# Cross-attention in 160 slots: the path of the probabilities from block transposes to key rows, and the buffers of z and x

## The chip, the cores and the metric

The kernel runs on one core of a Trainium2 chip. The metric is device microseconds (us) of one execution. A profile of one execution stands beside it; its span runs from the core's first to its last instruction.

## The reference

`x` holds 32 batches of 512 rows (queries) by 640 channels, `ctx` holds 32 batches of 77 rows (keys) by 1024. There are 20 heads of 32 channels. The other three key groups of the reference (object, others, ip) begin behind row 77, so they are empty here and add nothing. What is left:

```
q = heads(x @ to_q_w); k = heads(ctx @ to_k_w); v = heads(ctx @ to_v_w)
p = softmax(q @ k.T / sqrt(32)); a = merge(p @ v)
out = a @ to_out_w + to_out_b + x
```

All inputs and outputs are float32.

## The kernel before, in words

**Precision.** The large products (queries, keys, values, output) run in the faster fp32r form. Each operand is split into a high part (cast, ScalarE) and a low part (difference, VectorE or GpSimd), and three products (high-high, high-low, low-high; `PAIRS`) are summed. Scores and probabilities times values run in plain fp32.

**Stages.** First come 12 products of zeros (`warm`, line 253) while the first weights arrive. Then keys and values of all batches are computed in five groups of context rows and stored to DRAM (`k_dram`, `v_dram`). Then the main part runs as 160 slots: slot n is batch b = n // 5 and channel chunk j = n % 5, that is four heads of one batch. `end()` closes the last batches.

**One slot** (`slot`, line 573). The order on each engine is the order in which the program writes the instructions (a manual schedule), so each engine and the DMA-issuing queue of SyncE (SP) go through their own list in order, and an instruction that waits holds up all behind it on that engine.

- TensorE: `scores(n)` (line 410, `sc`), `values(n-3)` (line 478, `pa` from `raw` and `vb`), a piece of the output projection (line 515, `po`), `queries(n+1)` (line 393, `pq`), a second piece of the projection. Batch 0 and slots 5 and 6 have no projection pieces (`has_out` is false); slots 0 to 6 are called the filling here.
- VectorE: `maxima` (line 422), `transpose_p(n-1)` (line 454), additions of the residual (line 544), block transposes of x (line 235), the reciprocal of the sums (line 442), the low part of `pa` (line 497).
- ScalarE: 16 exponentials with sums (line 432, `pn`), the high part of `pa`, the copy of `pq` (line 402), the high parts of x (line 242).
- GpSimd: bias (line 508), normalization of `pn` (line 447), the low parts of x (line 243).

**The way of the probabilities.** `pn` holds queries in the partitions. The values product needs keys in the partitions. `transpose_p(n-1)` turns 32x32 blocks with VectorE into the one buffer `z`: partition 32a+i of `z` holds row i of every block, for the queries of block a. A row of 80 columns per head does not begin at a multiple of 32, so blocks straddle heads. Four transfers on SP (line 461, 160 KB each) write `z` to a DRAM buffer `pd` (`pd<-z`). One slot later `load_p` (line 470) reads it back with one 640 KB transfer (`raw<-pd`), whose 80 partitions are the keys. `raw` has two buffers and is read by `values` a slot after that.

**The way of x.** `load_x` (line 231) loads a batch in four transfers of 320 KB into `xs`, of which there is one buffer. Slots j = 0 and 1 of a batch turn the next batch's `xs` in place (line 235), slots j = 2 and 3 split it into `xt` (lines 242 and 243; seven buffers of one chunk each). In the steady part the load of batch b+2 stands at the end of that, in slot j = 4, since it has to wait until the splits have read `xs`. On SP it stands ahead of that slot's stores of `z`.

Of the kernel before, what the change touches and what calls it, by code (L numbers as in the profile page):

```python
# [8 lines left out]
F32 = mybir.dt.float32  # L9
# [14 lines left out]
P = 128  # L24
Q = 32
# [1 line left out]
HD = 32  # L27
NKEY = 77
HPC = 4
KPAD = 80  # L30
NBLK = HPC * KPAD // Q

# [3 lines left out]
def kernel(  # L38
# [43 lines left out]

    k_dram = dram.tile([P, NC_, NT], F32, name="k_dram")

    v_dram = dram.tile([NT + KPAD - NKEY, NC_, HPC, HD], F32, name="v_dram")
    wo_dram = dram.tile([P, NC_, 2, C], FPR, name="wo_dram")

    def split(hi, lo, src):
# [135 lines left out]
    def load_x(b, quarters=range(4)):  # L224

        if b not in xss:
            xss[b] = xpool[0].tile([P, S // Q, C // 4], F32, tag="xs", name="xs")
        xs = xss[b]
        src = x[b].rearrange("(a j) (q u) -> q j a u", j=Q, q=4)
        for q in quarters:  # L230
            nc.sync.dma_start(xs[q * Q : (q + 1) * Q, :, :], src[q])  # L231

    def transpose_x(b, i):
        part = xss[b][:, 4 * i : 4 * i + 4, :].rearrange("p a u -> p (a u)")
        nc.vector.transpose(part, part)  # L235

    def split_x(b, c, high=nc.scalar.copy, low=nc.gpsimd):

        xt = xpool[0].tile([P, 2, S], FPR, tag="xt", name="xt", bufs=7)
        src = xss[b].rearrange("p (a t) u -> p t a u", t=NQ)[:, :, :, c * Q : (c + 1) * Q]  # L240
        parts = [xt[:, i, :].rearrange("p (t a j) -> p t a j", t=NQ, j=Q) for i in range(2)]
        high(parts[0], src)  # L242
        low.tensor_tensor(parts[1], src, parts[0].bitcast(F32), ALU.subtract)  # L243
        xts[b, c] = xt
# [4 lines left out]
    zero = kvt.tile([P, G], FPR, name="zero")  # L249
    nc.vector.memset(zero.bitcast(F32), 0.0)  # L250
    warm = psk.tile([P, G], F32, tag="ps", name="warm")
    for _ in range(12):
        nc.tensor.matmul(warm, zero[:, :P], zero, start=True, stop=True)

    def first(*ks):
# [38 lines left out]
    def split_wo():  # L294
# [6 lines left out]
    load_context(1, NK)  # L301
    nc.sync.dma_start(
        v_dram[NT:].rearrange("n j i d -> (n j i d)").rearrange("(p u) -> p u", p=P),
        zero[:, : (KPAD - NKEY) * HEADS * HD // P].bitcast(F32),
    )
    for g in range(LAST):
        for j in range(NC_):
# [54 lines left out]


    main = ctx.enter_context(tc.tile_pool(name="main", bufs=1, reuse_waits="tile"))
    ps = ctx.enter_context(tc.tile_pool(name="ps", bufs=1, space=PSUM, reuse_waits="tile"))
    psv = tc.alloc_tile_pool(name="psv", bufs=3, space=PSUM, side="right", reuse_waits="tile")
    late = []

    raws, ats, pds, sms, pqs, pas, xrs, pos, scs, nms, rss = ({} for _ in range(11))

    bias = main.tile([P, C], F32, name="bias")
    nc.sync.dma_start(bias, bo.unsqueeze(0).to_broadcast([P, C]))
    kbs = [main.tile([P, NC_, NKEY], F32, name=f"kb{n}") for n in range(2)]
    vbs = [main.tile([KPAD, NC_, HPC, HD], F32, name=f"vb{n}") for n in range(2)]
    pnb = []
    for n in range(2):
        pn = main.tile([P, NQ * HPC, KPAD], F32, name=f"pn{n}")
        nc.gpsimd.memset(pn, 0.0)
        pnb.append(pn)
    qts = [main.tile([P, S], F32, name=f"qt{n}") for n in range(2)]  # L380
    z = main.tile([P, NBLK, NQ, Q], F32, name="z")
    def load_keys(b):
        nc.sync.dma_start(kbs[b % 2], k_dram[:, :, b * NKEY : (b + 1) * NKEY])

    def load_values(b):
        nc.sync.dma_start(vbs[b % 2], v_dram[b * NKEY : b * NKEY + KPAD])

    def queries(n):
        b, j = divmod(n, NC_)
        pqs[n] = ps.tile([P, S], F32, tag="pq", name="pq", bufs=1)  # L390
        for k in range(NC_):
            for m, (a, c) in enumerate(PAIRS):
                nc.tensor.matmul(  # L393
                    pqs[n],
                    wq_s[:, k, a, j * P : (j + 1) * P],
                    xts[b, k][:, c, :],
                    start=(k == 0 and m == 0),
                    stop=(k == NC_ - 1 and m == 2),
                )
# [37 lines left out]
                accum_out=sms[n][:, at : at + 1],  # L437
            )

    def sums(n):  # L440
        rss[n] = main.tile([P, NQ * HPC], F32, tag="rs", name="rs", bufs=2)
        nc.vector.reciprocal(rss[n], sms.pop(n))  # L442

    def normalize(n):
        rs = rss.pop(n)
        pf = pnb[n % 2][:, :, :NKEY]
        nc.gpsimd.tensor_tensor(  # L447
            pf, pf, rs.unsqueeze(2).to_broadcast([P, NQ * HPC, NKEY]), ALU.mult
        )

    def transpose_p(n):

        pn = pnb[n % 2]
        nc.vector.transpose(  # L454
            z.rearrange("p b t j -> p t b j"),
            pn.rearrange("p (t h) k -> p t (h k)", t=NQ).rearrange("p t (b i) -> p t b i", i=Q),
        )
        pd = dram.tile([NBLK * Q, S], F32, tag="pd", name="pd", bufs=6)
        rows = pd.rearrange("(b i) q -> i b q", i=Q)
        for a in range(4):  # L460
            nc.sync.dma_start(  # L461
                rows[:, :, a * P : (a + 1) * P],
                z[a * Q : (a + 1) * Q].rearrange("p b t j -> p b (t j)"),
            )
        pds[n] = pd

    def load_p(n):
        pd = pds.pop(n)
        raw = late[0].tile([KPAD, HPC, S], F32, tag="raw", name="raw", bufs=2)
        nc.sync.dma_start(raw, pd.rearrange("(h k) q -> k h q", h=HPC))  # L470
        raws[n] = raw

    def values(n):
# [64 lines left out]
    def finish():  # L538

        while closed:  # L540
            b, t, h = closed.pop(0)
            xr = xrs[b, t]
            cols = slice(h * HALF, (h + 1) * HALF)
            nc.vector.tensor_tensor(  # L544
                xr[:, cols], pos.pop((b, t, h))[:, :HALF], xr[:, cols], ALU.add
            )
            if (b, t) == (B - 1, NQ - 1):
                nc.sync.dma_start(out[b, t * P : (t + 1) * P, cols], xr[:, cols])
            elif h == 1:
                nc.sync.dma_start(out[b, t * P : (t + 1) * P, :], xr)  # L550
# [8 lines left out]
    PIECES = {2: (1, 0), 3: (1, 2), 4: (1, 4), 0: (2, 6), 1: (2, 8)}  # L559
    RESIDUAL = {1: (1, 0), 2: (1, 1), 3: (1, 2), 4: (1, 3)}  # L560
    BIAS = {2: (1, 0), 3: (1, 1), 4: (1, 2), 0: (2, 3)}
    TRANSPOSE_X = {0: ((0,), (1,)), 1: ((2,), (3,))}
    SPLIT_X = {2: (0, 1), 3: (2, 3, 4)}

    WO = {1: (0, 1, 2), 2: (3,), 3: (4,)}
# [7 lines left out]
    def slot(n, beside=()):  # L573
        b, j = divmod(n, NC_)
        ahead, more = n + 1 < N, b + 1 < B
        back, first = PIECES[j]
        bo_, has_out = b - back, b >= back
        xsplits = SPLIT_X.get(j, ()) if more and n > LATE else ()
        turns = TRANSPOSE_X.get(j, ((), ())) if more and b else ((), ())
        if b == 1 and j < 2:  # L580
            turns = (((), ()), ((0, 1), (2, 3)))[j]
        taken = takes.get(n)
        filling = not has_out

        scores(n)
        if taken is not None:
            values(taken)
        maxima(n)
        if n - LAG + 1 in pds and n > LATE:
            load_p(n - LAG + 1)  # L590
        for k in WO.get(n, ()):
            nc.sync.dma_start(wos[0][:, k].bitcast(F32), wo_dram[:, k].bitcast(F32))
        if j == 0 and more:
            load_keys(b + 1)
        if j == 1:
            load_values(b)
        if n == NC_:
            load_x(b + 1, (2, 3))
        if j == 4 and b and b + 2 < B:
            load_x(b + 2, (0, 1))  # L600
        if j in RESIDUAL and b >= RESIDUAL[j][0]:
            load_residual(b - RESIDUAL[j][0], RESIDUAL[j][1])
        if j in BIAS and b >= BIAS[j][0]:
            add_bias(b - BIAS[j][0], BIAS[j][1])
        if has_out:
            piece(bo_, first)
        for i in range(2):
            exps(n, i)
        if n:
            transpose_p(n - 1)  # L610
        finish()
        if j == 4 and b + 2 < B:
            load_x(b + 2, (0, 1) if not b else (2, 3))
        for i in turns[0]:
            transpose_x(b + 1, i)
        if len(beside) > 1:
            context_values(LAST, beside[1], psv)
        if ahead:
            queries(n + 1)
        if len(beside) > 0:  # L620
            context_values(LAST, beside[0], psv)
        if filling and ahead:
            copy_q(n + 1, nc.vector.tensor_copy)
        for i in range(2, HPC):
            exps(n, i)
        sums(n)
        normalize(n)
        if taken is not None:
            high_a(taken)
        if has_out and ahead:  # L630
            copy_q(n + 1)
        if has_out:
            piece(bo_, first + 1)
        if taken is not None:
            low_a(taken)
        for c in xsplits:
            split_x(b + 1, c)
        for i in turns[1]:
            transpose_x(b + 1, i)
        finish()  # L640

    def end():


        last = B - 1
        load_p(N - 2)
        add_bias(last - 1, 3)
        piece(last - 1, 6)
        finish()
        transpose_p(N - 1)  # L650
        load_p(N - 1)
        load_residual(last, 0)
        load_residual(last, 1)
        piece(last - 1, 7)
        finish()
        take(N - 3)
        piece(last - 1, 8)
        piece(last - 1, 9)
# [63 lines left out]
    late.append(  # L722
        ctx.enter_context(tc.tile_pool(name="psl", bufs=1, space=PSUM, reuse_waits="tile"))
    )
    load_p(0)
    for n in range(LATE, N):
        slot(n)
    end()
# [40 lines left out]
```

## Time and profile before

| | |
|---|---|
| median of 3 runs | 1810.46 us (1807.93 to 1810.99) |
| the profiled execution | 1809.79 us, its span 1808.0 us |
| TensorE, share of the span busy | 98% |
| VectorE, ScalarE, GpSimd | 52%, 61%, 44% |
| transfers of `pd<-z`, `raw<-pd` | 640 and 160 |

In the rows, PE is TensorE, PEld its weight loads, DVE is VectorE, ACT is ScalarE, POOL is GpSimd, SP is SyncE; a q behind the name is the engine's instruction queue (SPq issues transfers). `out<-in` are tiles, x3840 is a count, `128x320` is partitions by elements. In rows of waits, "A <- B: 19.6, 17, 3.1" says that A stood idle until B released it, 19.6 us in total, 17 times, at most 3.1 us. In the timeline a row has start, length, engine, line, and in brackets the idle time before it and what ended it; neighbouring instructions of one kind are merged. In the chain of waits a row has start, length and what the end of the program was waiting for at that time. A window row has the bounds, then each engine's busy time and count, the granted TensorE clock (1.00 is full) and the DMA engines' busy share and GB/s.

### The profile page before, as it was taken

To read this page: it belongs to the slowest core of one execution; us is meant where nothing else is said; L and a number is where in the kernel's file an instruction comes from. 1 tells how busy PE (TensorE), PEld (TensorE's weight loads), DVE (VectorE), ACT (ScalarE), POOL (GpSimd) and SP (SyncE) were. 2 spreads that over 40 slices of the span, in tenths; PEclk is the share of its full clock that TensorE was granted. 3 is DMA by queue.
4 is the path that set the end of the run, shared out by engine and by line. 5 is a ranking of instruction groups with operands and counts; after the bars stand their busy time and mean duration, and the time that the engine had idled before them with its cause. 6 is when DMAs were issued, how large, how long until landed. Compare 5 with 4: busy or idle time off the path is not lost.

```text
span 1808.0 us, 39341 instructions
## 1 busy us (share of the span) xinstructions
PE 1763.3 (98%) x13852; PEld 1440.0 (80%) x13852; DVE 933.3 (52%) x1651; ACT 1108.9 (61%) x5698; POOL 789.7 (44%) x502
## 2 busy tenths in 40 slices
PE   8999998899999999999999999999999999999999
PEld 7888896678878888877788777888788888877787
DVE  5233134555555555555555555555555555545553
ACT  3132035666767777767677776677676777666662
POOL 0000034444445555545555545545555555535453
PEclk9999999999999999999999999999999999999999
DMA  9746465899999999998999999998899999898987
GB/s 186 149 94 174 105 168 138 211 231 235 232 232 239 232 243 235 240 235 219 237 232 237 228 230 237 230 233 230 229 234 230 229 240 237 229 224 219 236 207 202
DMA packets 465173, 389.12 MB, mean 215 GB/s; under 512 B 91280, under 2 KB 372368, under 8 KB 464976
## 3 DMA queue, kind: packets, MB, share of 16 engines
q1 hardware_dynamic: 462384, 379.49, 84.5%
q0 software_dynamic: 2496, 6.97, 1.3%
q8 instruction: 109, 1.79, 0.4%
q14 instruction: 88, 0.72, 0.1%
q10 hardware_dynamic: 96, 0.16, 0.0%
HBM read 223.82 MB, written 162.70 MB: 214 GB/s over the span
## 4 chain that ended last, share of the span: by engine, by line
PE 63%; DMA 17%; ACT 6%; POOL 6%; SPq 4%; DVE 2%; issue 2%; POOLq 0%; DVEq 0%; ACTq 0%
PE po L515 20%; PE pq L393 17%; PE pk L177 7%; PE pv L177 7%; DMA raw<-pd 6%; DMA pd<-z 6%; ACT pn L432 6%; PE sc L410 5%; PE pa L478 5%; POOL xt L243 4%; DMA xs<-in_x_dram 4%; SPq L461 2%; POOL pn L447 1%; SPq L231 1%; DVE xs L235 1%
## 5 line engine op out<-in xcount | busy, mean ns | idle before, releaser
L432 ACT ACTIVATE pn<-sc,nm 128x77 f32<-128x77 f32 x2560 | 787.4, 361 | 400.2 <-DVE nm L422 379.6
L515 PEld LDWEIGHTS po<-wo_s,at 128*128 128x128 f32 x3840 | 582.7, 190 | 143.8 <-issue 132.1
L447 POOL TENSOR_TENSOR pn<-pn,rs 128x1232 f32<-128x1232 f32 x160 | 364.0, 2275 | 665.1 <-DVE rs L442 659.9
L515 PE MATMUL po<-wo_s,at 128*128 128x320 f32 x3840 | 636.8, 316 | 0.0
L432 ACT ACTIVATION_READ_ACCUMULATOR pn<-sc,nm 128x1 f32 x2560 | 618.7, 242 | 0.0
L393 PE MATMUL pq<-xt,wq_s 128*128 128x512 f32 x2400 | 582.8, 395 | 0.0
L393 PEld LDWEIGHTS pq<-xt,wq_s 128*128 128x128 f32 x2400 | 450.1, 190 | 92.8 <-issue 4.9
L422 DVE TENSOR_REDUCE nm<-sc 128x4 f32<-128x308 f32 x640 | 261.0, 469 | 202.2 <-PE sc L410 202.1
L454 DVE STREAM_TRANSPOSE z<-pn 128x1280 f32<-128x1280 f32 x160 | 241.1, 1507 | 97.8 <-DMA pd<-z 92.3
L508 POOL TENSOR_TENSOR xr<-xr,bias 128x640 f32<-128x640 f32 x128 | 200.8, 1569 | 94.2 <-DMA xr<-in_x_dram 85.9
L243 POOL TENSOR_TENSOR xt<-xs,xt 128x512 fp32r<-128x512 f32 x160 | 200.0, 1274 | 35.6 <-ACT xt L242 35.6
L478 PE MATMUL pa<-raw,vb 80*32 80x512 f32 x1280 | 173.4, 613 | 27.6 <-DMA raw<-pd 19.6
L410 PEld LDWEIGHTS sc<-kb,qt 32*128 32x128 f32 x5120 | 157.5, 186 | 41.0 <-issue 35.1
L410 PE MATMUL sc<-kb,qt 32*128 32x77 f32 x5120 | 181.0, 277 | 8.7 <-DVE rs L442 5.8
L544 DVE TENSOR_TENSOR xr<-po,xr 128x320 f32<-128x320 f32 x256 | 117.5, 469 | 79.4 <-PE po L515 75.7
L235 DVE STREAM_TRANSPOSE xs<-xs 128x640 f32<-128x640 f32 x128 | 105.8, 832 | 74.2 <-DMA xs<-in_x_dram 74.2
L442 DVE RECIPROCAL rs<-sm 128x16 f32<-128x16 f32 x160 | 38.8, 243 | 196.3 <-ACT pn L432 196.3
L177 PE MATMUL pk<-ct,wk_s 128*128 128x512 f32 (+1 forms) x600 | 136.0, 387 | 3.1 <-ACT wk_s L89 3.1
L402 ACT COPY qt<-pq 128x512 f32<-128x512 f32 x153 | 93.3, 610 | 72.5 <-PE pq L393 72.1
L177 PE MATMUL pv<-ct,wv_s 128*128 128x512 f32 (+1 forms) x600 | 133.9, 381 | 0.0
L177 PEld LDWEIGHTS pk<-ct,wk_s 128*128 128x128 f32 x600 | 114.2, 191 | 23.2 <-ACT wk_s L89 3.6
L497 DVE TENSOR_TENSOR at<-pa,at 128x512 fp32r<-128x512 f32 x160 | 108.6, 679 | 37.2 <-ACT at L492 37.1
(31 smaller groups left out, 536.7 us busy)
## 6 DMA issues: line engine op xcount, KB each, us to landing
pd<-z SPq DMA_DIRECT2D x640, 160.0 KB, 5.4
raw<-pd SPq DMA_DIRECT2D x160, 640.0 KB, 5.5
xs<-in_x_dram SPq DMA_DIRECT2D x128, 320.0 KB, 6.0
xr<-in_x_dram SPq DMA_DIRECT2D x128, 320.0 KB, 5.7
out_dram<-xr SPq DMA_DIRECT2D x127, 320.0 KB, 3.9
vb<-v_dram SPq DMA_DIRECT2D x32, 200.0 KB, 6.0
kb<-k_dram SPq DMA_DIRECT2D x32, 192.5 KB, 7.3
cs<-in_ctx_dram SPq DMA_DIRECT2D x12, 512.0 KB, 9.4
```

Source lines behind the costliest of these rows:

```text
L177: nc.tensor.matmul(held[j][:, :gn], w[:, k, a, :], cts[g, k][:, c, :gn], start=(k == 0 and n == 0), stop=(k == NK - 1 and n == 2),)
L235: nc.vector.transpose(part, part)
L243: low.tensor_tensor(parts[1], src, parts[0].bitcast(F32), ALU.subtract)
L393: nc.tensor.matmul(pqs[n], wq_s[:, k, a, j * P : (j + 1) * P], xts[b, k][:, c, :], start=(k == 0 and m == 0), stop=(k == NC_ - 1 and m == 2),)
L410: nc.tensor.matmul(sc[:, t, :NKEY], qts[n % 2][r, t * P : (t + 1) * P], kbs[b % 2][r, j, :], start=True, stop=True, tile_position=(i * HD, 0),
L422: nc.vector.tensor_reduce(nms[n][:, i], sc[:, :, :NKEY], AX.X, ALU.max, negate=True)
L432: nc.scalar.activation(pnb[n % 2][:, at, :NKEY], sc[:, t, :NKEY], AF.Exp, bias=nms[n][:, i, t : t + 1], accum_out=sms[n][:, at : at + 1],)
L447: nc.gpsimd.tensor_tensor(pf, pf, rs.unsqueeze(2).to_broadcast([P, NQ * HPC, NKEY]), ALU.mult)
L454: nc.vector.transpose(z.rearrange("p b t j -> p t b j"), pn.rearrange("p (t h) k -> p t (h k)", t=NQ).rearrange("p t (b i) -> p t b i", i=Q),)
L478: nc.tensor.matmul(pas[n][i * HD : (i + 1) * HD, :], vb[:, i, :], raw[:, i, :], start=True, stop=True, tile_position=(0, i * HD),)
L508: nc.gpsimd.tensor_tensor(xrs[b, t], xrs[b, t], bias, ALU.add)
L515: nc.tensor.matmul(pos[b, t, h][:, :HALF], ats[b * NC_ + j][:, a, t * P : (t + 1) * P], wos[0][:, j, c, h * HALF : (h + 1) * HALF], start= ...
```

## The change

- A head's row of `pn` grows from 80 to 96 columns (`KPAD`), three blocks of 32 (`KBLK`), so that no block straddles heads. `z` becomes two buffers, used in turn, laid out by head, block, query block.
- `pd`, its four stores and its load go. `move_p(n-1)` takes their place in slot n: twelve transfers on SP, SBUF to SBUF, one for each block row c (keys 32c to 32c+31, 16 rows in the last) and query block a. Eight carry 64 KB and four carry 32 KB, all in runs of 512 bytes. They stand behind the first additions and stores of the output in the slot.
- `xs` has two buffers. Batch b+2 is loaded one transfer per slot, in j = 1 to 4. The chunks 2 to 4 of odd batches have three `xt` buffers of their own (`xu`), and those of batch 1 are split in slots 0 to 2. The transposes of x are no longer spread over two places in a slot.
- In the filling, `values` stands behind `queries` instead of ahead.
- The products of zeros at the start go from 12 to 22.

The core of the diff:

```diff
-KPAD = 80
-NBLK = HPC * KPAD // Q
+KROW = 80
+KPAD = 96
+KBLK = KPAD // Q
...
-            xss[b] = xpool[0].tile([P, S // Q, C // 4], F32, tag="xs", name="xs")
+            xss[b] = xpool[0].tile([P, S // Q, C // 4], F32, tag="xs", name="xs", bufs=2)
...
-        xt = xpool[0].tile([P, 2, S], FPR, tag="xt", name="xt", bufs=7)
+        if b % 2 and c > 1:
+            xt = xpool[1].tile([P, 2, S], FPR, tag="xu", name="xu", bufs=3)
+        else:
+            xt = xpool[0].tile([P, 2, S], FPR, tag="xt", name="xt", bufs=7)
...
-    for _ in range(12):
+    for _ in range(22):
         nc.tensor.matmul(warm, zero[:, :P], zero, start=True, stop=True)
...
-    z = main.tile([P, NBLK, NQ, Q], F32, name="z")
+    zs = [main.tile([P, HPC, KBLK, NQ, Q], F32, name=f"z{n}") for n in range(2)]
...
     def transpose_p(n):
-        pn = pnb[n % 2]
+        pn, z = pnb[n % 2], zs[n % 2]
         nc.vector.transpose(
-            z.rearrange("p b t j -> p t b j"),
+            z.rearrange("p h c t j -> p t (h c) j"),
             pn.rearrange("p (t h) k -> p t (h k)", t=NQ).rearrange("p t (b i) -> p t b i", i=Q),
         )
-        pd = dram.tile([NBLK * Q, S], F32, tag="pd", name="pd", bufs=6)
-        rows = pd.rearrange("(b i) q -> i b q", i=Q)
-        for a in range(4):
-            nc.sync.dma_start(
-                rows[:, :, a * P : (a + 1) * P],
-                z[a * Q : (a + 1) * Q].rearrange("p b t j -> p b (t j)"),
-            )
-        pds[n] = pd
-
-    def load_p(n):
-        pd = pds.pop(n)
-        raw = late[0].tile([KPAD, HPC, S], F32, tag="raw", name="raw", bufs=2)
-        nc.sync.dma_start(raw, pd.rearrange("(h k) q -> k h q", h=HPC))
+
+    def move_p(n):
+
+        z = zs[n % 2]
+        raw = late[0].tile([KROW, HPC, S], F32, tag="raw", name="raw", bufs=2)
+        for c in range(KBLK):
+            rows = min(Q, KROW - c * Q)
+            for a in range(4):
+                nc.sync.dma_start(
+                    raw[c * Q : c * Q + rows, :, a * P : (a + 1) * P],
+                    z[a * Q : a * Q + rows, :, c].rearrange("i h t j -> i h (t j)"),
+                )
         raws[n] = raw
...
-    TRANSPOSE_X = {0: ((0,), (1,)), 1: ((2,), (3,))}
+    TRANSPOSE_X = {0: (0, 1), 1: (2, 3)}
...
-        xsplits = SPLIT_X.get(j, ()) if more and n > LATE else ()
+        xsplits = (SPLIT_X if b else {0: (2,), 1: (3,), 2: (4,)}).get(j, ()) if more else ()
...
         scores(n)
-        if taken is not None:
+        if taken is not None and has_out:
             values(taken)
         maxima(n)
-        if n - LAG + 1 in pds and n > LATE:
-            load_p(n - LAG + 1)
+        if n:
+            transpose_p(n - 1)
...
-        if n == NC_:
-            load_x(b + 1, (2, 3))
-        if j == 4 and b and b + 2 < B:
-            load_x(b + 2, (0, 1))
+        if b + 2 < B:
+            quarters = {4: (0, 1), 5: (2, 3)}.get(n, ()) if n <= NC_ else (j - 1,) if j else ()
+            if quarters:
+                load_x(2 if n <= NC_ else b + 2, quarters)
...
-        if n:
-            transpose_p(n - 1)
         finish()
-        if j == 4 and b + 2 < B:
-            load_x(b + 2, (0, 1) if not b else (2, 3))
-        for i in turns[0]:
+        if n >= LATE:
+            move_p(n - 1)
+        for i in turns:
             transpose_x(b + 1, i)
...
         if ahead:
             queries(n + 1)
+        if taken is not None and not has_out:
+            values(taken)
```

In `end()`, `transpose_p(N - 1)` moves to the front and `move_p(N - 1)` stands ahead of `take(N - 3)`; `move_p(0)` stands where `load_p(0)` stood, ahead of slot 2.

More of the change, by code (lines that the diff above doesn't have):

```diff
@@ L83 @@
     k_dram = dram.tile([P, NC_, NT], F32, name="k_dram")
-    v_dram = dram.tile([NT + KPAD - NKEY, NC_, HPC, HD], F32, name="v_dram")
+    v_dram = dram.tile([NT + KROW - NKEY, NC_, HPC, HD], F32, name="v_dram")
     wo_dram = dram.tile([P, NC_, 2, C], FPR, name="wo_dram")
@@ L303 @@
         v_dram[NT:].rearrange("n j i d -> (n j i d)").rearrange("(p u) -> p u", p=P),
-        zero[:, : (KPAD - NKEY) * HEADS * HD // P].bitcast(F32),
+        zero[:, : (KROW - NKEY) * HEADS * HD // P].bitcast(F32),
     )
@@ L364 @@
     main = ctx.enter_context(tc.tile_pool(name="main", bufs=1, reuse_waits="tile"))
+    xpool.append(main)
     ps = ctx.enter_context(tc.tile_pool(name="ps", bufs=1, space=PSUM, reuse_waits="tile"))
@@ L367 @@
     late = []
-    raws, ats, pds, sms, pqs, pas, xrs, pos, scs, nms, rss = ({} for _ in range(11))
+    raws, ats, sms, pqs, pas, xrs, pos, scs, nms = ({} for _ in range(9))
     bias = main.tile([P, C], F32, name="bias")
@@ L373 @@
     kbs = [main.tile([P, NC_, NKEY], F32, name=f"kb{n}") for n in range(2)]
-    vbs = [main.tile([KPAD, NC_, HPC, HD], F32, name=f"vb{n}") for n in range(2)]
+    vbs = [main.tile([KROW, NC_, HPC, HD], F32, name=f"vb{n}") for n in range(2)]
     pnb = []
@@ L385, in load_values @@
     def load_values(b):
-        nc.sync.dma_start(vbs[b % 2], v_dram[b * NKEY : b * NKEY + KPAD])
+        nc.sync.dma_start(vbs[b % 2], v_dram[b * NKEY : b * NKEY + KROW])
     def queries(n):
@@ L438, in exps @@
             )
-    def sums(n):
-        rss[n] = main.tile([P, NQ * HPC], F32, tag="rs", name="rs", bufs=2)
-        nc.vector.reciprocal(rss[n], sms.pop(n))
     def normalize(n):
-        rs = rss.pop(n)
+        rs = main.tile([P, NQ * HPC], F32, tag="rs", name="rs", bufs=2)
+        nc.vector.reciprocal(rs, sms.pop(n))
         pf = pnb[n % 2][:, :, :NKEY]
@@ L577, in slot @@
         bo_, has_out = b - back, b >= back
-        xsplits = SPLIT_X.get(j, ()) if more and n > LATE else ()
-        turns = TRANSPOSE_X.get(j, ((), ())) if more and b else ((), ())
+        xsplits = (SPLIT_X if b else {0: (2,), 1: (3,), 2: (4,)}).get(j, ()) if more else ()
+        turns = TRANSPOSE_X.get(j, ()) if more and b else ()
         if b == 1 and j < 2:
-            turns = (((), ()), ((0, 1), (2, 3)))[j]
+            turns = ((), range(NQ))[j]
         taken = takes.get(n)
-        filling = not has_out
         scores(n)
-        if taken is not None:
+        if taken is not None and has_out:
             values(taken)
         maxima(n)
-        if n - LAG + 1 in pds and n > LATE:
-            load_p(n - LAG + 1)
+        if n:
+            transpose_p(n - 1)
         for k in WO.get(n, ()):
@@ L619, in slot @@
             queries(n + 1)
+        if taken is not None and not has_out:
+            values(taken)
         if len(beside) > 0:
             context_values(LAST, beside[0], psv)
-        if filling and ahead:
+        if ahead and not has_out:
             copy_q(n + 1, nc.vector.tensor_copy)
@@ L625, in slot @@
             exps(n, i)
-        sums(n)
         normalize(n)
@@ L637, in slot @@
             split_x(b + 1, c)
-        for i in turns[1]:
-            transpose_x(b + 1, i)
         finish()
@@ L645, in end @@
         last = B - 1
-        load_p(N - 2)
+        transpose_p(N - 1)
         add_bias(last - 1, 3)
@@ L649, in end @@
         finish()
-        transpose_p(N - 1)
-        load_p(N - 1)
         load_residual(last, 0)
@@ L655, in end @@
         finish()
+        move_p(N - 1)
         take(N - 3)
@@ L724 @@
     )
-    load_p(0)
+    move_p(0)
     for n in range(LATE, N):
```

## The prediction

> **What bounds the kernel now.** I read the page's engine table first, then the timeline of TensorE, then the waits, and last the chain of waits around one lost stretch.
>
> ```profile
> PE 1763.3 (98%) x13852; PEld 1440.0 (80%) x13852; DVE 933.3 (52%) x1651; ACT 1108.9 (61%) x5698; POOL 789.7 (44%) x502
> ```
>
> TensorE is the bound: no engine beside it is over 61%. What can be won is its idle time, and the matmuls that run slower after an idle stretch. The timeline of TensorE shows a slot that loses nothing, and the start of one that does:
>
> ```profile
> 412.74 1.13 PE L410 MATMUL sc<-kb,qt 32*128 32x77 f32 x32
> ...
> 414.80 2.02 PE L515 MATMUL po<-wo_s,at 128*128 128x320 f32 x12
> 416.66 3.59 PE L393 MATMUL pq<-xt,wq_s 128*128 128x512 f32 x15
> ...
> 421.94 1.13 PE L410 MATMUL sc<-kb,qt 32*128 32x77 f32 x32
> 423.50 1.06 PE L478 MATMUL pa<-raw,vb 80*32 80x512 f32 x8 [0.43 <-DMA raw<-pd]
> ```
>
> Scores start at 412.74 and again at 421.94: 9.2 us, most slots 9.19, in which no row has an idle time. The second slot waits at `pa` for `raw`. The same rows at slot 8, the first beyond the filling that runs freely, and at the last slot, 159:
>
> ```profile
> 345.17 1.13 PE L410 MATMUL sc<-kb,qt 32*128 32x77 f32 x32
> ...
> 1770.00 1.13 PE L410 MATMUL sc<-kb,qt 32*128 32x77 f32 x32
> ```
>
> 151 slots take 1424.8 us; 151 x 9.19 is 1387.7. So **37.1 us** are lost in the steady part. Nearly all of it is in front of `pa` in slots j = 1, and the worst case shows why it is more than the wait:
>
> ```profile
> 1598.67 1.83 PE L478 MATMUL pa<-raw,vb 80*32 80x512 f32 x8 [3.06 <-DMA raw<-pd]
> 1600.43 3.57 PE L515 MATMUL po<-wo_s,at 128*128 128x320 f32 x12
> 1603.80 4.49 PE L393 MATMUL pq<-xt,wq_s 128*128 128x512 f32 x15
> ```
>
> After 3.06 us of waiting, `po` takes 3.57 instead of 2.02 and `pq` 4.49 instead of 3.59. The chain of waits behind the stall at 939 us says what makes `raw` late there:
>
> ```profile
> 919.48 3.77 POOL xt L243 x3
> ...
> 923.26 0.32 SPq L231
> ...
> 924.71 0.43 SPq L461
> ...
> 926.24 5.87 DMA pd<-z
> ...
> 932.18 6.83 DMA raw<-pd
> ...
> 939.14 1.07 PE pa L478 x8
> ```
>
> The loads of x wait on SP until GpSimd has split the old x; the stores of `z` stand behind them in the queue; then come a store to DRAM and a read back. From the first store's issue (924.71) to `pa` are 14.4 us. The waits, of the engines and then of SP's own queue, have the same links:
>
> ```profile
> DVE z L454 <- DMA pd<-z: 92.3, 78, 5.5
> ```
> ```profile
> SPq L231 <- POOL xt L243: 67.8, 30, 3.2
> ```
>
> 30 waits of SP, one a batch, match the place j = 4, 0, 1.
>
> **The change part by part.**
>
> *Steady part.* With a second `xs`, the load of batch b+2 goes into a buffer whose splits ended a batch earlier, so the SP wait (67.8 us) goes, and with it VectorE's wait for x (74.2 us, in the row of line 235 below). With a second `z`, VectorE's 92.3 us go. The DRAM trip goes. What is late next? I follow one slot:
>
> ```profile
> 956.47 1.13 PE L410 MATMUL sc<-kb,qt 32*128 32x77 f32 x32
> ...
> 959.17 1.50 DVE L454 STREAM_TRANSPOSE z<-pn 128x1280 f32<-128x1280 f32 x1
> ```
>
> The transpose starts 2.7 us into the slot. It grows from 1280 to 1536 elements: 1.50 x 1.2 = 1.8 us, so `z` is ready at +4.5. VectorE, busy 52%, takes the 0.3 us between `maxima` and the reciprocal, which waits for ScalarE anyway. Then SP issues twelve transfers instead of four and one. Their price from SP's timeline:
>
> ```profile
> 1235.59 1.88 SPq L461 DMA_DIRECT2D pd<-z  x4
> ...
> 1243.61 2.92 SPq L461 DMA_DIRECT2D pd<-z  x4
> ```
>
> With a free queue a store costs 1.88 / 4 = 0.47 us, with a full one 2.92 / 4 = 0.73. No transfer from SBUF to SBUF is in this trace. I bound its issue from below by the 0.30 us of `raw<-pd` below and from above by 0.94 (18.82 us for 20 transfers of 64 KB):
>
> ```profile
> 55.16 18.82 SPq L216 DMA_DIRECT2D v_dram<-vs  x20
> ...
> 1234.02 0.30 SPq L470 DMA_DIRECT2D raw<-pd  x1
> ```
>
> I take 0.48. The 0.73 belongs to a queue that gets 160 KB per issue; the new transfers bring 64 KB or less, and the DMA engines have less to move: 640 KB a slot for the probabilities instead of 1280. Their speed alone is bounded by the stores, in a stretch with little else:
>
> ```profile
> 281.25 2.21 SPq L461 DMA_DIRECT2D pd<-z  x4
> ```
> ```profile
> GB/s 0 0 0 0 0 0 0 64 183 183 179 183 179 179 171 167 184 166 188 183 149 98 73 94 145 231 290 309 284 286 308 92 222 111 55 0 32 64 137 235
> ...
> pd<-z SPq DMA_DIRECT2D x4, 160.0 KB, 3.1
> ```
>
> At some 180 GB/s, in the same 512-byte runs, 64 KB take 0.36 us, less than one issue, so no queue builds up. Twelve issues then take 5.8 us, and the last lands some 3.1 us later: `raw` is complete at +4.5 + 5.8 + 3.1 = +13.4. It is read two slots on, at 2 x 9.19 + 1.06 = +19.4. Six us of cover; the stall goes. The buffer `raw` is free in time, since `values(n-3)` reads it within the first 2.1 us. SP in total: 12 x 0.48 plus 2.8 others (loads of x and residual, stores of the output, keys, values: 128 + 128 + 127 + 32 + 32 over 160 slots) x 0.5 makes 7.2 of 9.19 us. So **-37.1**. If the cover is gone, at most these 37.1 stay and more comes (rivals).
>
> The Trainium skill, "DMA: Bandwidth & Descriptors", Rules for kernel authors, says to coalesce small transfers, since under 64 KB one pays mostly overhead; its section on the anatomy of a DMA gives about 2.0 us fixed per transfer (for the GpSimd path). If these ran one after another, twelve would make some 26 us a slot, an estimate from that page. The row above speaks against it: four transfers, issued in 2.21 us, landed 3.1 us each after issue, so they overlap.
>
> *Filling.* Slot 2 starts at 290.40, slot 3 at 297.64, slot 8 at 345.17. Between them `pa` waits for `raw`:
>
> ```profile
> 290.40 1.13 PE L410 MATMUL sc<-kb,qt 32*128 32x77 f32 x32 [1.38 <-DVE rs L442]
> ...
> 297.64 1.13 PE L410 MATMUL sc<-kb,qt 32*128 32x77 f32 x32 [0.87 <-DVE qt L402]
> ...
> 308.38 1.77 PE L478 MATMUL pa<-raw,vb 80*32 80x512 f32 x8 [2.39 <-DMA raw<-pd]
> ```
>
> Slots 2 to 7 take 54.8 us. An undisturbed one takes 297.64 - 290.40 = 7.24: scores, first maximum, the exponentials, scores again. Without waiting for `raw`, slots 2 to 5 take 4 x 7.24 = 29.0. Slot 6 has four transposes of x ahead of the copy of `pq`:
>
> ```profile
> L235 DVE STREAM_TRANSPOSE xs<-xs 128x640 f32<-128x640 f32 x128 | 105.8, 832 | 74.2 <-DMA xs<-in_x_dram 74.2
> ...
> L402 ACT COPY qt<-pq 128x512 f32<-128x512 f32 x153 | 93.3, 610 | 72.5 <-PE pq L393 72.1
> ```
>
> With `z` ready at +4.5, 4 x 0.83 and 0.61 it comes to some 8.7; slot 7 is a full one, 9.2. Together 46.9: **-8.0**. Bounds: 0, if twelve issues a slot (5.8 of 7.24 us) are late as the store is now, and -10.
>
> *Start.* Ten more products of zeros:
>
> ```profile
> 1.46 4.58 PE L253 MATMUL warm<-zero 128*128 128x512 f32 x12 [1.46 <-DVE zero L250]
> ...
> 9.14 0.82 DVE L90 TENSOR_TENSOR wk_s<-wraw,wk_s 128x640 fp32r<-128x640 f32 x1 [0.35 <-DMA cs<-in_ctx_dram]
> 9.16 6.43 PE L177 MATMUL pk<-ct,wk_s 128*128 128x512 f32 x15 [3.12 <-ACT wk_s L89]
> ...
> 17.49 3.56 PE L177 MATMUL pk<-ct,wk_s 128*128 128x512 f32 x15
> ```
> ```profile
> 10.00:15.00 5.00, 5.00 (x13) 3.93 (x13) 3.74 (x7) 1.96 (x4) 0.00 (x0) 0.50 0.94 191
> ```
>
> Now 3.12 us of idling lead to a clock of 0.50 and to 6.43 instead of 3.56 us. The twelve take 4.58 us and end at 6.04; ten more at the same 0.38 or less end at 9.8 at the latest, so the gap closes. 2.87 us come free, less 0.4 in which the third product waits for the low half of the weights (ready at 9.96). **-2.5**, bounds +0.7 and -2.9.
>
> *Sum*, against the profiled execution's 1809.8 (span 1808.0; the median of the runs is 0.7 above it): 1809.8 - 37.1 - 8.0 - 2.5 = **1762**. The tail keeps its order on TensorE, and its last `raw` has some 3 us to spare.
>
> **The rivals.**
>
> *Slower: SP becomes the bound.* Place: `move_p` in each slot. SP's 12 t + 1.4 reaches 9.19 at t = 0.65 us; beyond it each slot grows. At 0.70 a slot takes 9.80: 1762 + 151 x 0.61 = **1854**. It eats the whole gain at t = 0.675. For it: the stores now cost 0.73 in a full queue. Against it: the same stores cost 0.47 in a free one, and the queue gets emptier. The Trainium skill, "Perfetto Trace Analysis", What "DMA-bound" means, counts a sequencer solid with transfers as a bound of its own; no stretch of this trace shows SP solid.
>
> *Half.* Order on SP keeps some of the stall (moves behind an output store that waits for VectorE): half of 37.1 stays, **1781**.
>
> *Waits on TensorE.* `pa` must wait for twelve transfers. Each further wait is an instruction of its own, 51 ns; `z` now needs two for its four transfers:
>
> ```profile
> L478 PEldq EVENT_SEMAPHORE  x160: 51/51/682, 297.9 to 1791.6; - x160
> ```
> ```profile
> L454 DVEq EVENT_SEMAPHORE  x318: 49/50/2048, 291.7 to 1779.5; - x159
> ```
>
> By that ratio five more, 0.26 us a slot if nothing hides them: **1801**; with eleven more, 1847. Against it: the 1.06 us of scores ahead of `pa` hide them; that is why I take 0.
>
> *No effect.* The stall at `pa` stays with another cause, VectorE's longer transpose say: **about 1810**.
>
> **How the numbers follow.** Forecast 0.58 (its own range 1756 to 1775), half 0.12, TensorE's waits 0.08 (0.02 of it slower), no effect 0.06, SP the bound 0.13, slower in some other way 0.03. Within 0.2% (3.6 us, about what a measurement can tell) gets 0.07, slower 0.18, faster 0.75. The range goes from 1756 (all lower bounds, rounded down) to 1815 and leaves out SP as the bound, the slower waits and the rest: 0.18.
>
> **What would show it.** Right: no idle time before `pa` with `raw` as releaser, slots of 9.19 throughout, SP issues near 0.48, the first `pk` group near 3.6 us, slot 8 at about 335. Wrong: slots evenly longer than 9.19 with SP issuing without a pause, or a `pa` that is late in every slot.

## The result, and the profile after

| | before | after |
|---|---|---|
| median | 1810.72 us | 1901.1 us |
| ratio, 95% interval | | 1.0504 (1.0485 to 1.0522) |
| profiled execution, span | 1808.0 us | 1898.0 us |

Slower by 5%, where 2.7% faster was forecast. The span is cut at the starts of scores (line 415 after, line 410 before):

| stretch | before | after | difference | forecast |
|---|---|---|---|---|
| to slot 0 | 264.62 | 262.10 | -2.5 | -2.5 |
| slots 0 to 7 | 80.55 | 83.24 | +2.7 | -8.0 |
| 151 slots, 8 to 158 | 1424.83 | 1507.82 | +83.0 | -37.1 |
| slot 159 and the tail | 38.0 | 44.9 | +6.9 | 0 |

The mean slot of the steady part went from 9.44 to 9.985 us; 9.19 is a slot without loss. The page after: engines, the main queue (packets, MB, share of 16 engines), the shares of the chain that ended last, and the new transfers (KB each, us to landing).

```profile
PE 1806.9 (95%) x13862; PEld 1468.2 (77%) x13862; DVE 979.1 (52%) x1651; ACT 1113.1 (59%) x5698; POOL 792.5 (42%) x502
...
q1 hardware_dynamic: 429104, 274.70, 62.2%
...
PE 71%; SPq 17%; DMA 6%; issue 2%; DVE 2%; POOL 1%; ACT 1%; DVEq 0%; POOLq 0%; ACTq 0%
...
raw<-z SPq DMA_DIRECT2D x1280, 64.0 KB, 3.2
...
raw<-z SPq DMA_DIRECT2D x640, 32.0 KB, 2.0
```

The DMA engines have less to do (this queue had 84.5% before), the transfers land in 2 to 3.2 us, and still a sixth of the chain is SP issuing. The timeline of SP after, somewhat more than one slot (start, length):

```profile
1006.69 8.90 SPq L468 DMA_DIRECT2D raw<-z  x12
1015.63 0.58 SPq L232 DMA_DIRECT2D xs<-in_x_dram  x1
1016.26 0.49 SPq L505 DMA_DIRECT2D xr<-in_x_dram  x1
1016.85 0.36 SPq L551 DMA_DIRECT2D out_dram<-xr  x1
1017.32 7.76 SPq L468 DMA_DIRECT2D raw<-z  x12
1025.12 0.59 SPq L388 DMA_DIRECT2D kb<-k_dram  x1
1025.83 8.28 SPq L468 DMA_DIRECT2D raw<-z  x12
```

There is no pause: each row begins where the one before ends. That is the row to look for in a queue that is the bound. The instructions of the line (least, median, longest ns):

```profile
L468 SPq DMA_DIRECT2D raw<-z x1920: 585/599/2097, 286.5 to 1880.0; - x192
```

The chain of waits shows how TensorE pays: twelve issues in a row, a landing of 2 us, then `pa`.

```profile
945.87 0.59 SPq L468
...
953.39 0.59 SPq L468
...
954.02 1.99 DMA raw<-z
...
956.21 1.07 PE pa L479 x8
```

The 160 groups of twelve take 7.65 to 9.80 us, mean 8.28, or 0.69 us a transfer with the step to the next instruction. Summed over the trace from slot 8 to slot 159, 1507.8 us, SP is in issues for 1374 us: 7.7 us a slot in the twelve (0.642 each in the mean), 1.4 in the others. It steps from one instruction to the next in some 0.04 us, and all its pauses of more than 0.15 us make 16 us together. SP sets the pace.

### The profile page after: what moved, and what is told of

It is laid out like the page before. It is cut to its first block, busy times and chain, and to the rows that moved or that the text cites. A ratio compares the mean times of both kernels' runs of the same rounds, so it can differ in the third digit from the quotient of the medians.

```text
span 1898.0 us, 41325 instructions
## 1 busy us (share of the span) xinstructions
PE 1806.9 (95%) x13862; PEld 1468.2 (77%) x13862; DVE 979.1 (52%) x1651; ACT 1113.1 (59%) x5698; POOL 792.5 (42%) x502
## 4 chain that ended last, share of the span: by engine, by line
PE 71%; SPq 17%; DMA 6%; issue 2%; DVE 2%; POOL 1%; ACT 1%; DVEq 0%; POOLq 0%; ACTq 0%
PE po L516 23%; PE pq L398 21%; SPq L468 16%; PE pv L178 7%; PE pk L178 7%; PE pa L479 7%; PE sc L415 6%; DMA xr<-in_x_dram 3%; DMA raw<-z 2%; DVE nm L427 1%; DMA xs<-in_x_dram 1%; SPq L232 1%; ACT pn L437 1%; SPq L551 0%; POOL pn L449 0%
## 5 line engine op out<-in xcount | busy, mean ns | idle before, releaser
L516 PEld LDWEIGHTS po<-wo_s,at 128*128 128x128 f32 x3840 | 598.4, 195 | 156.1 <-issue 139.3
L516 PE MATMUL po<-wo_s,at 128*128 128x320 f32 x3840 | 654.5, 321 | 3.6 <-DVE xr L545 3.6
L398 PE MATMUL pq<-xt,wq_s 128*128 128x512 f32 x1680 | 428.5, 403 | 0.0
L398 PEld LDWEIGHTS pq<-xt,wq_s 128*128 128x128 f32 x1680 | 322.5, 196 | 61.4
L456 DVE STREAM_TRANSPOSE z<-pn 128x1536 f32<-128x1536 f32 x160 | 283.0, 1769 | 14.2 <-DMA raw<-z 8.4
L479 PE MATMUL pa<-raw,vb 80*32 80x512 f32 x1280 | 179.2, 631 | 69.8 <-DVE nm L427 44.3
L398 PE MATMUL pq<-xu,wq_s 128*128 128x512 f32 x720 | 182.3, 397 | 0.0
L398 PEld LDWEIGHTS pq<-xu,wq_s 128*128 128x128 f32 x720 | 136.5, 190 | 33.2
L247 POOL TENSOR_TENSOR xt<-xs,xt 128x512 fp32r<-128x512 f32 x112 | 139.8, 1273 | 38.7 <-ACT xt L246 38.7
```

The source lines that it names most:

```text
L398: nc.tensor.matmul(pqs[n], wq_s[:, k, a, j * P : (j + 1) * P], xts[b, k][:, c, :], start=(k == 0 and m == 0), stop=(k == NC_ - 1 and m == 2),)
L456: nc.vector.transpose(z.rearrange("p h c t j -> p t (h c) j"), pn.rearrange("p (t h) k -> p t (h k)", t=NQ).rearrange("p t (b i) -> p t b ...
L479: nc.tensor.matmul(pas[n][i * HD : (i + 1) * HD, :], vb[:, i, :], raw[:, i, :], start=True, stop=True, tile_position=(0, i * HD),)
L516: nc.tensor.matmul(pos[b, t, h][:, :HALF], ats[b * NC_ + j][:, a, t * P : (t + 1) * P], wos[0][:, j, c, h * HALF : (h + 1) * HALF], start= ...
```

## The experiments

Theory: SP's issues are the bound, at a price per transfer that hangs on its kind. Rivals: the bytes or the runs between SBUF and SBUF; TensorE's waits on twelve transfers; the way through DRAM, which the prediction held harmless but for the loads of x in front of it. Kernels of one group shared a chip; the kernel before took 1795.92 us in the first group (e1 to e4), 1804.41 in the second (e5 to e8), 1804.9 in the third (e9, e10). e1, e2, e3, e7 and e8 were executed once each, so their times come without an interval; the changed kernel itself was run again in the second group only (e8). A mean slot is worked out as above, from slot 8 to slot 159.

### e1_eight: eight transfers instead of twelve

```diff
-        for c in range(KBLK):
-            rows = min(Q, KROW - c * Q)
+        for c in range(2):
+            rows = Q
...
-                vb[:, i, :],
-                raw[:, i, :],
+                vb[: 2 * Q, i, :],
+                raw[: 2 * Q, i, :],
```

> The changed kernel with eight transfers a slot instead of twelve: the third block row (keys 64 to 76) is left out of the move and of the values product. Theory (SyncE's queue is the bound, 0.60 to 0.64 us per issue whatever it carries): 8 x 0.64 + 1.4 = 6.5 us of 9.19, so the loss goes, slots of 9.2, 1762 to 1772 us. Rival 1 (the bytes between SBUF and SBUF are the bound): four fifths of the bytes stay, some 1880 us. Rival 2 (TensorE's waits on many transfers): the number of waits is the same or a third less, 1870 us or more.

1775.4 us, span 1773.6. The issues still take 599 ns, but SP now pauses between the groups:

```profile
1014.34 5.10 SPq L468 DMA_DIRECT2D raw<-z  x8
1019.66 0.41 SPq L551 DMA_DIRECT2D out_dram<-xr  x1
1020.11 0.45 SPq L232 DMA_DIRECT2D xs<-in_x_dram  x1
1020.60 1.54 SPq L505 DMA_DIRECT2D xr<-in_x_dram  x1
1023.53 5.11 SPq L468 DMA_DIRECT2D raw<-z  x8
```

From 1022.14 to 1023.53 SP waits for `z`. The mean slot is 9.22, against 9.44 in the kernel before, and no slot of the steady part is longer than 9.27. So 32 of the 37 us were there to be had. TensorE's part got no lighter: `pa` has fewer rows (64 instead of 80) and takes 1.06 us as before. The time misses the expected 1772 by 3 us: the tail still takes 44.3 us.

### e2_quarter_bytes: twelve transfers, one head of four

```diff
-        raw = late[0].tile([KROW, HPC, S], F32, tag="raw", name="raw", bufs=2)
+        raw = late[0].tile([KROW, 1, S], F32, tag="raw", name="raw", bufs=2)
...
-                    z[a * Q : a * Q + rows, :, c].rearrange("i h t j -> i h (t j)"),
+                    z[a * Q : a * Q + rows, :1, c].rearrange("i h t j -> i h (t j)"),
...
-                raw[:, i, :],
+                raw[:, 0, :],
```

> The changed kernel with the same twelve transfers, but each moves only the first of its four heads, 16 KB instead of 64 (all four values products read that head, so three heads get other probabilities). Theory (price per issue): nothing changes, 1885 to 1902 us, issues of 0.60 us. Rival 1 (bytes, or number of 512-byte runs): a quarter of either, 1762 to 1775 us and issues near 0.45 us.

1851.94 us, between the two expectations and nearer to the theory. The issue's median hardly moves:

```profile
L468 SPq DMA_DIRECT2D raw<-z x1920: 507/588/1691, 286.6 to 1831.8; - x192
```

A group of twelve takes 7.97 us in the mean instead of 8.28, the mean slot is 9.70 instead of 9.985 (10.03 in e8; neither was measured in this group). With a quarter of the bytes and of the runs, 0.5 us of a loss of 0.8 stays. The median price is per transfer: in the changed kernel itself, too, the transfers of 32 KB are issued in 593 ns and those of 64 KB in 599. The longer issues stay as frequent with fewer bytes, 123 over 0.7 us here and 122 there.

### e3_2kb_runs: the same bytes in runs of 2 KB

```diff
-    zs = [main.tile([P, HPC, KBLK, NQ, Q], F32, name=f"z{n}") for n in range(2)]
+    zs = [main.tile([P, KBLK, NQ * HPC, Q], F32, name=f"z{n}") for n in range(2)]
...
-            z.rearrange("p h c t j -> p t (h c) j"),
-            pn.rearrange("p (t h) k -> p t (h k)", t=NQ).rearrange("p t (b i) -> p t b i", i=Q),
+            z.rearrange("p c n j -> p n c j"),
+            pn.rearrange("p n (c i) -> p n c i", i=Q),
...
-                    raw[c * Q : c * Q + rows, :, a * P : (a + 1) * P],
-                    z[a * Q : a * Q + rows, :, c].rearrange("i h t j -> i h (t j)"),
+                    raw[c * Q : c * Q + rows, a].rearrange("k n j -> k (n j)"),
+                    z[a * Q : a * Q + rows, c].rearrange("k n j -> k (n j)"),
```

(`raw` has the matching layout, and `values` reads it with a stride.)

> The changed kernel with z and raw laid out by block row and query block, so that each transfer is 32 runs of 2 KB instead of 128 of 512 bytes; same bytes, same twelve issues, same result. Theory (a fixed price per issue between SBUF and SBUF): 1885 to 1902 us, issues of 0.60 us. Rival (the price of an issue goes by its runs or by its dimensions): issues near 0.45 us as those of z to DRAM before, 12 x 0.49 + 1.4 = 7.3 us of 9.19, 1762 to 1775 us.

1874.94 us, 10 below the expected range, mean slot 9.83. The median issue is the same to 11 ns, 588 against 599; only the first of each group is cheaper (513 against 591), in e2 as well. So neither the number of runs nor the number of dimensions sets the price.

### e4_dram: the rest of the change without the move

```diff
-    def move_p(n):
-        ... (twelve transfers)
+    def store_p(n):   # four stores to DRAM, as before
+    def load_p(n):    # one load, one slot later, as before
...
+        if n > LATE:
+            load_p(n - 2)
...
-        finish()
-        if n >= LATE:
-            move_p(n - 1)
+        if n:
+            store_p(n - 1)
+        finish()
```

> The rest of the change without the move: two buffers of z and of x, the spread loads, the order of the filling, 22 products at the start, but the probabilities go through DRAM with four stores and one load a slot as before. Theory (the stall before came from the loads of x in front of the stores on SyncE's queue, and the loss after from the issues alone): SyncE has 8.8 issues a slot fewer than after... that is 5 + 2.8 instead of 14.8, the stall goes, slots of 9.19 from slot 8 on, 1762 to 1772 us. Rival (the way through DRAM is late by itself): the stall before pa stays, 1795 to 1811 us.

1844.03 us, ratio 1.0278 (1.0231 to 1.0326): slower than before, against theory and rival. The waits, of SP's queue and then of the engines:

```profile
SPq L476 <- DMA pd<-z: 604.7, 320, 7.3
```
```profile
PE pa L484 <- DMA raw<-pd: 32.5, 41, 3.2
```

SP waits 605 us for the stores to land before it may issue the load; before it were these:

```profile
SPq L470 <- DMA pd<-z: 385.3, 304, 4.7
```

The stores land after 6.4 us (5.4 before), with one load of x and one of the residual ahead of them in most slots, and whatever stands behind the load on SP, the next loads and stores, waits with it. The stall is now spread over all slots (mean 9.61). So the way through DRAM is late also when the loads of x are spread and wait for no split, and the edits beside the move, taken together, made it worse. Which of them did most of that was not separated.

### e5_pool_queue: the third block row from GpSimd's queue

```diff
-                nc.sync.dma_start(
+                (nc.gpsimd if c == 2 else nc.sync).dma_start(
...
-        transpose_p(N - 1)
         add_bias(last - 1, 3)
         piece(last - 1, 6)
         finish()
+        transpose_p(N - 1)
```

> The changed kernel, all twelve transfers, but the four of 32 KB (keys 64 to 79) are issued by GpSimd instead of SyncE; and in the tail the last transpose of the probabilities stands behind the first additions of the output again, as in the kernel before. Theory (SyncE's issues are the bound, 0.62 us each): SyncE has 8 x 0.62 + 1.4 = 6.4 us a slot, slots of 9.2 us; GpSimd takes four issues of 0.65 us into some 5 us of idle time a slot. Some 6 us come back in the tail. 1765 to 1775 us, below both kernels. Rival 1 (TensorE's waits on twelve transfers, or the landing): still 1830 us or more. Rival 2 (GpSimd becomes late): stalls at pa or in the scores, 1790 to 1850 us.

1773.65 us, ratio 0.9831 (0.9809 to 0.9853): with all twelve transfers 1.7% faster than the kernel before, and 7% faster than the changed one (e8). The windows of this kernel (busy time of PE, PEld, DVE, ACT, POOL; clock, DMA share, GB/s) and its issues:

```profile
900.00:1100.00 200.00, 199.91 (x1723) 161.69 (x1722) 119.43 (x204) 141.69 (x757) 147.52 (x147) 1.00 0.70 166
```
```profile
L468 SPq DMA_DIRECT2D raw<-z x1280: 585/599/2035, 286.9 to 1751.3; - x183
...
L468 POOL DMA_DIRECT2D raw<-z x640: 512/512/552, 293.8 to 1746.0; - x160
```

TensorE is busy for 199.91 of 200 us at a clock of 1.00. GpSimd takes 0.51 us for an issue in time it had free. The Trainium skill, "Perfetto Trace Analysis", DMA Optimizations, says that balancing transfers over the engines may help when an engine looks busy with descriptor generation; with GpSimd the rows agree, with ScalarE (e6) they do not.

### e6_act_queue: the third block row from ScalarE's queue

```diff
-                nc.sync.dma_start(
+                (nc.scalar if c == 2 else nc.sync).dma_start(
```

(and the tail as in e5)

> As the kernel with GpSimd's queue, but ScalarE issues the four transfers of 32 KB, between the first two and the last two heads' exponentials. Theory: SyncE is free as there; ScalarE's chain in a slot grows from 6.8 to some 8.6 to 9.2 us (4 issues of 0.46 to 0.62), at the edge of the slot: 1765 to 1800 us. Rival (waits or landing): 1830 us or more.

2141.26 us, ratio 1.1874 (1.1841 to 1.1908), against both. SP is free here, but ScalarE stops between its exponentials:

```profile
L468 ACTq DMA_DIRECT2D raw<-z x640: 592/609/2212, 286.8 to 2108.4; - x160
```
```profile
ACT pn L437 <- DMA raw<-z: 380.1, 111, 7.2
```

Two things are to be seen. An issue from ScalarE costs nearly the same, 0.61 us, so the price is not SP's own. And the expectation forgot that a transfer on ScalarE makes its exponentials wait for `z` and for earlier transfers: the slot's longest chain, with no cover.

### e7_twelve_stores: the kernel before, its four stores cut into twelve

```diff
-            nc.sync.dma_start(
-                rows[:, :, a * P : (a + 1) * P],
-                z[a * Q : (a + 1) * Q].rearrange("p b t j -> p b (t j)"),
-            )
+            for b0, b1 in ((0, 4), (4, 8), (8, 10)):
+                nc.sync.dma_start(
+                    rows[:, b0:b1, a * P : (a + 1) * P],
+                    z[a * Q : (a + 1) * Q, b0:b1].rearrange("p b t j -> p b (t j)"),
+                )
```

> The kernel before with its four stores of z to DRAM cut into twelve (blocks 0 to 3, 4 to 7, 8 and 9 of each query block; 64, 64 and 32 KB). What the issue of such a store takes tells whether the 0.60 us belong to transfers between SBUF and SBUF (then 0.45 to 0.50 us here when the queue is free) or to any transfer of that size in a row (then 0.58 to 0.62 us). Theory, the first; SyncE then has some 8 us of issues a slot and its wait for the stores to land on top, about 10 us: 1810 to 1900 us. By the second 1.4 us more a slot, 1900 us or more.

2146.78 us, mean slot 11.6: far above the first reading's range, and within the second's only because that has no upper end. The time decides nothing, but the issue does:

```profile
L462 SPq DMA_DIRECT2D pd<-z x1920: 302/432/2292, 281.2 to 2123.6; - x192
```
```profile
SPq L462 <- DMA raw<-pd: 246.7, 155, 2.9
```

A store of the same size to DRAM costs 0.43 us in the median, 0.60 belong to the transfers between SBUF and SBUF. Much of the rest is waiting: by the profile, stores stand on SP until an earlier `raw<-pd` has landed, a transfer whose data they do not touch. Why they do was not tried.

### e8_after_again

> The changed kernel once more, on the chip of this call, to stand beside the others: 5.0% above the kernel before, slots near 10.0 us.

1907.09 us, 5.7% above 1804.41, mean slot 10.03. Beside it e5 is 133 us shorter on the same chip.

### e9_two_xs: the kernel before with a second xs

```diff
-            xss[b] = xpool[0].tile([P, S // Q, C // 4], F32, tag="xs", name="xs")
+            xss[b] = xpool[0].tile([P, S // Q, C // 4], F32, tag="xs", name="xs", bufs=2)
```

> The kernel before with one edit: two buffers for the raw x (xs) instead of one; loads, stores and their order stay. The prediction's reading: the loads of x held up SyncE's queue until GpSimd had split the old x, and that made raw late in slots j = 1; without that wait the 37 us of the steady part mostly go, ratio 0.98 to 0.985. Rival (the way through DRAM, with DMA engines 92% busy, is late by itself and the wait only hid it): ratio 0.995 to 1.01, raw still late, in other slots.

Ratio 0.9999 (0.9979 to 1.0019). SP's wait for GpSimd (67.8 us before) is gone from its list, and a shorter one stands there; VectorE's wait for x stays:

```profile
SPq L231 <- DMA xs<-in_x_dram: 51.7, 55, 1.4
```
```profile
DVE xs L235 <- DMA xs<-in_x_dram: 74.0, 30, 5.3
...
PE pa L478 <- DMA raw<-pd: 12.4, 13, 2.5
```

`raw` is still late in slots j = 1: they take 10.08 us in the mean, 10.41 in the kernel before, and all others 9.2. The reading behind the forecast's largest term falls: the chain named the loads of x, but their wait was not what made `raw` late. The loads themselves still stand ahead of the stores here; what their bytes cost the way through DRAM was not tried by itself.

### e10_two_z: the kernel before with a second z

```diff
-    z = main.tile([P, NBLK, NQ, Q], F32, name="z")
+    zs = [main.tile([P, NBLK, NQ, Q], F32, name=f"z{n}") for n in range(2)]
...
-        pn = pnb[n % 2]
+        pn, z = pnb[n % 2], zs[n % 2]
```

> The kernel before with one edit: two buffers for z instead of one. VectorE's 92 us of waiting for the stores go. Theory: that wait was never on the path that sets the end, ratio 0.998 to 1.002. Rival: an earlier z lets the stores start earlier and takes off some of the stall at pa, ratio 0.985 to 0.995.

Ratio 1.0003 (0.9983 to 1.0023): VectorE's 92 us of waiting for the stores were on no path that sets the end.

## Why the prediction was wrong

The step that failed is the price of the issue: "I take 0.48". It came from stores to DRAM in a free queue. A transfer between SBUF and SBUF costs 0.60 us in the median and here never under 0.585, and 0.69 with the longer ones and the step to the next instruction counted. The sentence "64 KB take 0.36 us, less than one issue, so no queue builds up" was right for the DMA engines and did not matter. With 0.69 the prediction's own formula, 12 t + 1.4, gives 9.7 us, above 9.19: its rival "SP becomes the bound" came true, at 0.13. The text had the break-even (0.65) and two ends of the price around it (0.30 and 0.94), and chose the value that lay on the safe side by the nearest row of another kind.

The upper end was misread as well. The row of 18.82 us for 20 transfers of 64 KB merges two stretches of the kernel before, with 5.2 us between them in which SP issues nothing:

```profile
55.16 11.69 SPq L216 DMA_DIRECT2D v_dram<-vs  x16
```
```profile
72.05 1.93 SPq L216 DMA_DIRECT2D v_dram<-vs  x4
```

The sixteen took 0.73 us each, with single issues of up to 1.78 among them, and SP made no pause. So the sentence "no stretch of this trace shows SP solid" was wrong, and these transfers have the size of the new ones: at their 0.73 the formula gives 10.2 us a slot. The prediction's own 0.73, of the stores in a full queue, was set aside because those carry 160 KB; these carry 64.

The rival gave 1854 us for t = 0.70. The other 47: slots of 9.985 instead of 9.80 (28 us); the filling, +2.7 instead of -8.0 (11 us); the tail (7 us); the median, 1 us above the profiled execution. The twelve at 8.28 us and the others at 1.5 make the 9.8; for the rest, SP's waiting instructions and short pauses, the formula had no term.

- *Steady part, -37.1.* The size was nearly right: e1 and e5 have slots of 9.22 and 9.24, some 32 and 30 us less than before. The cause was wrong in two of three links: a second `xs` alone and a second `z` alone bring nothing (e9, e10). What goes with the move is the way through DRAM; e4 keeps that way with all else changed, and is late. The move without the rest was not tried.
- *Filling, -8.0.* The condition of the bound "0, if twelve issues a slot are late" is what happened, and +2.7 goes beyond that bound: slot 6 takes 15.25 us, because its loads of x stood on SP behind the twelve issues of 314.19 to 322.0 and were issued at 322.68, so that VectorE had x only at 328.54 and TensorE stood idle for 6.48 us ahead of the scores at 332.29. The products behind that idle time are slower (those scores 2.00 us instead of 1.13), and slot 7 takes 13.05. In e1 slot 8 starts at 336.6, near the 335 forecast, but by luck: slots 2 to 5 take 26.1 us there instead of the 29.0 forecast, slots 6 and 7 22.5 instead of 17.9.
- *Start, -2.5.* Right, to 0.1 us. The first two groups of products after:

```profile
1.46 7.46 PE L257 MATMUL warm<-zero 128*128 128x512 f32 x22 [1.46 <-DVE zero L254]
9.01 4.09 PE L178 MATMUL pk<-ct,wk_s 128*128 128x512 f32 x15
12.93 2.20 PE L178 MATMUL pv<-ct,wv_s 128*128 128x512 f32 x9
```

- *Tail, 0.* Wrong by 6.9 us. The order on TensorE is kept, but `transpose_p(N - 1)` now stands ahead of the additions on VectorE and starts only at 1863.08, when GpSimd has normalized the last probabilities (1862.60) and the last of the transfers that still read that `z` has landed (1862.70); the additions come behind it, the bank of the output is not free until then, and TensorE waits and is slower for a while after:

```profile
1855.22 6.43 PE L516 MATMUL po<-wo_s,at 128*128 128x320 f32 x42
1865.29 1.14 PE L516 MATMUL po<-wo_s,at 128*128 128x320 f32 x6 [3.64 <-DVE xr L545]
1866.36 1.94 PE L479 MATMUL pa<-raw,vb 80*32 80x512 f32 x8
1868.22 7.79 PE L516 MATMUL po<-wo_s,at 128*128 128x320 f32 x36
```

  In e5, with that one line moved back and the third block row on GpSimd's queue, the stretch from slot 159 takes 38.0 us again, and the 36 products 5.54. The shorter queue alone does not do it: in e1, with eight issues and the line where it is here, TensorE waits 3.21 us and the stretch takes 44.3.
- *TensorE's waits, taken as 0.* Nearly right. Slots that lose nothing else read 9.26 where they read 9.19 before; in e5 the mean is 0.05 us above 9.19, some 7 us in all. The extra waits are in the trace; that they are the cause was not tried by itself.

```profile
L479 PEldq EVENT_SEMAPHORE  x731: 51/51/3229, 296.7 to 1881.8; - x183
```

## What to carry to other kernels

When a change trades a few large transfers for many small ones, add up the issues of the queue over one period first, with a price for that very kind of transfer; if no row shows that kind, say at which price the queue becomes the bound, and time one such transfer before choosing a price below it. Before dividing a merged row of issues by its count, look whether it hides a pause. A stall that a chain of waits pins on one wait need not go with that wait: edit that wait alone before counting on it. When the issuing queue is the bound, an engine with free time in the right place can take part of the issues (e5), and the engine on the slot's longest chain cannot (e6).

## What the runs showed of the hardware

- An issue of a transfer between SBUF and SBUF takes 0.60 us on SP and 0.61 on ScalarE, 0.51 on GpSimd; stores of the same size to DRAM take 0.43 on SP in e7, and 0.50 where v is stored in the kernel before (64 KB each). These are medians. A quarter of the bytes or a quarter of the runs lowers SP's 0.60 by 0.01 us. What in the issue costs the difference of 0.10 to 0.17 stays open.
- Twelve issues in a row take 7.65 us at best and up to 9.80: single ones of 1 to 2 us are among them. Their cause was not settled; with a quarter of the bytes they are as frequent (e2), and they occur among stores to DRAM too (up to 2.29 us in e7).
